# Output gates on both row halves, router rows in spare score columns: the last stage of a four-layer kernel on one core

## The chip, the core and the metric

The kernel runs on one core of a Trainium2 chip. The metric is the device time in microseconds of one execution of the whole program; three runs of the kernel before gave 1846.86, 1848.22 and 1850.99 us, median 1848.22. Engines: TensorE (PE; its weight loads are PEld), VectorE (DVE), ScalarE (ACT), GpSimd (POOL), and SyncE (SP), which here issues DMA transfers. Each runs its own queue in order.

## The reference, cut to what matters

Four residual layers work on x [16, 256, 256] (batch, tokens, features). The first three (a cross attention, a mixture of eight experts, a second cross attention) are untouched by the change. The fourth is a gated linear attention with a dense part and a part routed over four experts:

```python
e = jax.nn.softmax(x @ We, axis=-1)                  # router: 4 experts
_, idx = lax.top_k(e, 1)
mask = jax.nn.one_hot(idx, N_EXP, dtype=x.dtype).sum(-2)
rw = e * mask
...
o = o_dense + o_sparse                               # chunks of 64 tokens, 8 heads of 64
g = (x @ Wga @ Wgb).reshape(B, L, H, DV)             # output gate, 64 wide inside
o = o * lax.rsqrt(jnp.mean(o * o, axis=-1, keepdims=True) + EPS) * norm_w
o = o * (g * jax.nn.sigmoid(g))
return o.reshape(B, L, H * DV) @ Wo
```

The change concerns three things in it: the second half of the output gate (`@ Wgb` and `g * sigmoid(g)`), the turning of the router's logits (`x @ We`) from rows to columns, and the place of one product with the values.

## The kernel before

The last stage is `stage3_fast` (line 1619). It goes through 16 batches; each batch has four slots, p = 4 b + m, and in slot m the heads 2m and 2m+1 are worked on. The slots are called 0 to 3 here. Work on the next batch is spread over the slots of this one. From the first slots on every engine takes its instructions in the order in which the program issues them (`x.tied = True`): nothing is rearranged. The order within a slot is written out in the loop over p at the end and in small tables, of which these matter:

```python
behind_mask = {0: [(route_logits, 1)]}
by_rows = {0: [(outgates, 0, 0)], 1: [(gates_end, 1)], 3: [(outgates, 0, 1)]}
logs = {0: [(route_sums, 1), (outgates_end, 0, 0)], 1: [(gate_logs, 1, 0)], 2: [(gate_logs, 1, 1), (norm_ahead, 2)],
        3: [(outgates_end, 0, 1)]}
...
inside = p % 4 in (1, 2) and p + 1 < last
```

An entry (f, d, ...) calls f for the batch d ahead. A slot runs: `masked(p - 1, 1)`, `keys_queries(p + 1)`, the tables `middle`, `rest`, `decays(p + 1)`, `late`, then `products(p, 0)` (first scores, sc<-f in the profile), `masked(p, 0)` on VectorE (at<-sc,amask), `behind_mask`, `factors(p + 1)`, `by_rows`; then, where `inside` holds, `summed(p)`, the product with the values of the slot before (o<-at,v); then `second(p + 1)` (gq<-low,lbk and gz<-low,lbk), `logs`, `products(p, 1)` (second scores, sc<-q,k), and, where `inside` does not hold, `summed(p)`.

Both score groups write the same two-bank PSUM tile sc (one buffer, 384 of 512 columns used in each bank): the second may only begin when the first has been read. A head pair uses both row halves of TensorE: one head has its data on partitions 0 to 63, the other on 64 to 127. All other PSUM tiles named by `bank(...)` rotate through two buffers.

The functions the change touches:

- `lows` (line 1688), in slot 0 for the next batch: a 256-row product low, copied out of PSUM by VectorE in four operations. Rows 0 to 63 of its second part are the gate's inner values; rows 64 to 127 hold the decay gates' inner values and, from row 81 on, the router's four rows.
- `route_logits` (line 1705), in slot 0 behind the masking: two TensorE transposes bring the router's rows into the bank rt; VectorE takes their maximum (emx) and subtracts it (e), ScalarE exponentiates. `route` follows in slot 1 with seven small VectorE operations, the last of which writes hot.
- `outgates` (line 1796) and `outgates_end` (line 1808): the gate's 512 columns in two calls of two 256-column matmuls each (zg<-low,lbg), in slots 0 and 3. Their operands lie on partitions 0 to 63, so they use TensorE's lower row half alone. ScalarE computes exp(-z) (eg<-zg), then Ln and Exp of it; VectorE copies z out (zs<-zg); GpSimd multiplies (gw<-zs,eg).
- `products` (line 1892), `masked` (line 1904), `values` (line 1922), `squares` (line 1937: ScalarE's sq<-o) and `gated` (line 1946: VectorE's u<-o,gw, issued after the squares of the same o).

Matmul lines read L1637 in the profile and transposes L1640, since helpers issue them; nearly all other operations read L50.

Of the kernel before, what the change touches and what calls it, by code (L numbers as in the profile page):

```python
# [10 lines left out]
F32 = mybir.dt.float32  # L11
I32 = mybir.dt.int32
AF = mybir.ActivationFunctionType
ALU = mybir.AluOpType
# [3 lines left out]
P = 128  # L18
B, S, D = 16, 256, 256
# [7 lines left out]
def bc(ap, shape, *axes):  # L27

    for a in axes:
        ap = ap.unsqueeze(a)  # L30
    return ap.to_broadcast(list(shape))
# [42 lines left out]
def layers(ctx: ExitStack, tc: tile.TileContext, t, out, check):  # L74
    nc = tc.nc
# [6 lines left out]
    def const(name, shape, dtype=F32):  # L82
        return cp.tile(list(shape), dtype, tag=name, name=name)
# [80 lines left out]
    ident = const("ident", [P, P])  # L164
# [12 lines left out]
    dve3, act3, pool3 = free = [Pinned(tc, x, False) for x in (nc.vector, nc.scalar, nc.gpsimd)]  # L177
# [694 lines left out]
    def w3_load(name, shape, src=None):  # L872
        x = c3(name, shape)
        src = t[src or name]
        weights.append((x, src if len(src.shape) == len(shape) else src.rearrange("(k p) f -> p k f", p=P)))
        return x
# [3 lines left out]
    lbg = w3_load("lbg", [P, 512])  # L880
# [738 lines left out]
    def stage3_fast(early_bank):  # L1619

        with ExitStack() as sx:
# [3 lines left out]
            def of(b):  # L1625

                return w1 if b % 2 else w0

            def bank(name):
                return pss.tile([P, 512], F32, tag="ps", name=name) if pss else early_bank(name)  # L1630

            def tokens(i):
                return slice(i * P, (i + 1) * P)


            def matmul(*a, **k):
                tc.keep_in_program_order(nc.tensor.matmul(*a, **k))  # L1637

            def transpose(*a):
                tc.keep_in_program_order(nc.tensor.transpose(*a))  # L1640
# [1 line left out]
            halves = w1.tile([P, P], F32, tag="halves", name="halves")  # L1642
            nc.sync.dma_start(out=halves, in_=t["halves"])

            lbg2 = w1.tile([64, 512], F32, tag="lbg2", name="lbg2")
            nc.sync.dma_start(out=lbg2, in_=t["lbg"][64:P, :])
            low2 = w1.tile([64, P], F32, tag="low2", name="low2")
            wo = w1.tile([P, 4, D], F32, tag="wo", name="wo")

            hots = [w1.tile([P, 2, 4], F32, tag=f"hot{n}", name=f"hot{n}") for n in range(2)]  # L1650

            xn, xnT, low, lg, hT, em, am = {}, {}, {}, {}, {}, {}, {}
            v, gw, u_, oT = {}, {}, {}, {}


# [32 lines left out]
            def lows(b):  # L1688

                low[b] = of(b).tile([P, 2, S], F32, tag="low", name="low")  # L1690
                ps = bank("low")
                for c in range(2):
                    for k in range(2):
                        matmul(ps[:, c * S:(c + 1) * S], la[:, k, c * P:(c + 1) * P], xnT[b][:, k, :],
                                         start=k == 0, stop=k == 1)
                dve3.tensor_copy(low[b][:, 0, :], ps[:, :S])
                dve3.tensor_scalar(low[b][:, 1, :], ps[:, S:], vec[:, V_ONE:V_ONE + 1], None, ALU.add)
                if b > 0:
                    for r in range(0, 64, 32):
                        dve3.tensor_scalar(low2[r:r + 32, :], ps[64 + r:96 + r, S + P:],  # L1700
                                           vec[64 + r:96 + r, V_ONE:V_ONE + 1], None, ALU.add)

            e_, den_, z_ = {}, {}, {}

            def route_logits(b):

                ps = bank("rt")
                for i in range(2):
                    transpose(ps[:, 64 * i:64 * i + 64], low[b][64:P, 1, tokens(i)], ident[64:P, 64:P])
                src = ps[:, :P].rearrange("p (i e) -> p i e", i=2)[:, :, 17:21]  # L1710
                mx = st.tile([P, 2], F32, tag="emx", name="emx")
                dve.tensor_reduce(mx, src, AX.X, ALU.max)
                e = e_[b] = st.tile([P, 2, 4], F32, tag="e", name="e")
                dve.tensor_tensor(e, src, bc(mx, [P, 2, 4], 2), ALU.subtract)
                act.activation(e, e, AF.Exp)

            def route_sums(b):
                den = den_[b] = st.tile([P, 2], F32, tag="eden", name="eden")
                dve.tensor_reduce(den, e_[b], AX.X, ALU.add)
                dve.reciprocal(den, den)  # L1720
# [72 lines left out]
                        matmul(ps, xnT[b][:, k, tokens(i)], wv3[:, k, :], start=k == 0, stop=k == 1)  # L1793
                    act3.copy(v[b][:, i, :], ps)

            def outgates(b, i):

                if i == 0:
                    gw[b] = w2.tile([P, 4, S], F32, tag="gw", name="gw")
                ps = bank("zg")  # L1800
                for m in range(2):
                    matmul(ps[:, m * S:(m + 1) * S], lbg[0:64, (2 * i + m) * P:(2 * i + m + 1) * P],
                           low[b][0:64, 1, :], start=True, stop=True)
                e = w2.tile([P, 512], F32, tag="eg", name="eg")
                act3.activation(e, ps, AF.Exp, scale=-1.0)
                z_[b, i] = ps, e

            def outgates_end(b, i):
                ps, e = z_.pop((b, i))
                zs = w2.tile([P, 512], F32, tag="zs", name="zs")  # L1810
                dve3.tensor_copy(zs, ps)
                act3.activation(e, e, AF.Ln, bias=1.0)
                act3.activation(e, e, AF.Exp, scale=-1.0)
                pool3.tensor_tensor(gw[b][:, 2 * i:2 * i + 2, :].rearrange("p m s -> p (m s)"), zs, e, ALU.mult)


            def place(p):
                b, m = p // 4, p % 4
                return b, m, slice(m * P, (m + 1) * P)
# [72 lines left out]
            def products(p, n):  # L1892

                b, m, cols = place(p)
                q, k = fq.pop((p, n)), fk.pop((p, n))
                ps = psa.tile([P, 2, 512], F32, tag="sc", name="sc")
                for lo, hi, i in ((0, S, 0), (P, S, 1)):
                    for j in range(2):
                        r = slice(64 * j, 64 * j + 64)
                        matmul(ps[:, j, lo + i * P:hi + i * P], k[r, tokens(i)], q[r, lo:hi],  # L1900
                                         start=True, stop=True)
                z_[p, n, "sc"] = ps
# [83 lines left out]
            def warm():  # L1986

                ps = bank("warm")
                for _ in range(2):
# [3 lines left out]
            start = {2: [(turn_hot, 1)]}  # L1993
# [3 lines left out]
            rest = {0: [(bias, 2)], 1: [(route, 1)], 2: [(steepest, 1, 0), (stats, 2)], 3: [(steepest, 1, 1), (turn_ahead, 2)]}  # L1997
            late = {1: [(scaled, -1, 1)], 2: [(project, -1)], 3: [(vals, 1)]}
            behind_mask = {0: [(route_logits, 1)]}
            by_rows = {0: [(outgates, 0, 0)], 1: [(gates_end, 1)], 3: [(outgates, 0, 1)]}  # L2000
            logs = {0: [(route_sums, 1), (outgates_end, 0, 0)], 1: [(gate_logs, 1, 0)], 2: [(gate_logs, 1, 1), (norm_ahead, 2)],
                    3: [(outgates_end, 0, 1)]}

            def run(steps, p):
                for f, d, *a in steps.get(p % 4, ()):
# [4 lines left out]
                x.tied = True  # L2010
            yield
            for group in (((bias, 0), (stats, 0)), ((norm, 0),), ((turn, 0),), ((lows, 0),), ((gates, 0, 0),),
                          ((gate_logs, 0, 0), (route_logits, 0)), ((route_sums, 0), (gates, 0, 1)),
                          ((route, 0), (vals, 0), (gate_logs, 0, 1), (bias, 1))):
                for f, *a in group:
                    f(*a)
                yield
# [6 lines left out]
            w1 = sx.enter_context(tc.tile_pool(name="f3w1", bufs=1, reuse_waits="tile"))  # L2024
            w2 = sx.enter_context(tc.tile_pool(name="f3w2", bufs=2, reuse_waits="tile"))
            psa = sx.enter_context(tc.tile_pool(name="f3psa", bufs=1, space=PSUM, reuse_waits="tile"))
            pss = sx.enter_context(tc.tile_pool(name="f3ps", bufs=2, space=PSUM, reuse_waits="tile"))
            last = 4 * B
            decays(0)
            for m in range(0, 3, 2):  # L2030
                ps = bank("k2")
# [12 lines left out]
            for p in range(last):  # L2044
                if p == 0:
                    turn(1)
                run(start, p)
                if p % 4 == 0:
                    shares(p // 4)
                if 0 < p:  # L2050
                    masked(p - 1, 1)
                run(copies, p)
                if p % 4 == 0:
                    shares_end(p // 4)
                if 1 < p and p % 2 == 1:
                    gated((p - 2) // 4, (p - 2) % 4 // 2)
                if p + 1 < last:
                    keys_queries(p + 1)
                run(middle, p)
                run(rest, p)  # L2060
                if p + 1 < last:
                    decays(p + 1)
                run(late, p)
                products(p, 0)
                masked(p, 0)
                run(behind_mask, p)
                if p + 1 < last:
                    factors(p + 1)
                run(by_rows, p)

                inside = p % 4 in (1, 2) and p + 1 < last
                if inside:
                    summed(p)
                if p + 1 < last:
                    second(p + 1)
                    factors_second(p + 1)
                run(logs, p)
                products(p, 1)
                if 0 < p and not inside:
                    summed(p)  # L2080

            b, p = B - 1, last - 1
# [126 lines left out]
```

## Time and profile before

| | |
|---|---|
| median of three runs | 1848.22 us |
| the profiled execution's own time | 1848.33 us |
| its span, first to last instruction | 1846.5 us |
| TensorE busy | 1818.5 us, 98% of the span |
| VectorE busy | 1253.5 us, 68% |
| GpSimd busy | 1017.4 us, 55% |
| ScalarE busy | 858.4 us, 46% |
| zg matmul passes in the last stage | 128, 388 ns each |
| zs copies on VectorE | 32, 676 ns each |
| one batch of the last stage, steady | 38.13 us (1500.06 to 1538.19) |

How to read the lines: a timeline row gives the start in us from the span's beginning, the time it covers, engine, line, operation, the tiles as out<-in, the shape of what is moved, and how many instructions are merged in it; in brackets, idle time of the engine before it and who ended it. A row with several matmuls covers all of them, and rows overlap where matmuls are in flight together, so the distance between two starts says more than a duration. Each fp32 matmul appears as two passes, so four matmuls are "x8". `rt` writes two transposes, one pass each. The table of slots gives busy microseconds of every engine in a stretch of time, with the number of instructions.

### The profile page before, as it was taken

The numbers are of one execution on the slowest core, as the hardware profiler recorded it, in microseconds if no ns is written. First come the engines' busy times: TensorE is split into PE (matmuls) and PEld (weight loads), VectorE is DVE, ScalarE is ACT, GpSimd is POOL, SyncE is SP. The second block draws the span as 40 slices with busy tenths as digits, with TensorE's granted clock in tenths as the row PEclk, the third lists the DMA queues.
The fourth block names the chain that finished last, engine by engine and source line by source line (L and its number), as shares of the span: only waits on it lengthen the run. The fifth ranks groups of instructions, "written<-read, shape, count | busy, mean of one in ns | idle before, by whom it ended". The sixth has DMA issues, their size and how long they took to land.

```text
span 1846.5 us, 35163 instructions
## 1 busy us (share of the span) xinstructions
PE 1818.5 (98%) x13870; PEld 1258.0 (68%) x13870; DVE 1253.5 (68%) x2935; ACT 858.4 (46%) x1772; POOL 1017.4 (55%) x1001
## 2 busy tenths in 40 slices
PE   8999999999999999999999999999999999999997
PEld 5666666666766667666777766667777777777775
DVE  3355656566665666656474488878888888888875
ACT  4433344433444334443433487754545545455452
POOL 4654767567676576756634766314444444444433
PEclk9999999999999999999999999999999999999999
DMA  9800010000010000000078933000000000000000
GB/s 297 233 1 22 17 34 15 25 17 23 23 37 10 27 19 10 31 25 15 15 249 240 227 47 51 15 1 5 9 7 7 7 12 7 7 7 7 13 7 14
DMA packets 67142, 84.67 MB, mean 46 GB/s; under 512 B 10467, under 2 KB 54611, under 8 KB 66457
## 3 DMA queue, kind: packets, MB, share of 16 engines
q1 hardware_dynamic: 54681, 65.56, 11.2%
q0 software_dynamic: 12288, 16.79, 4.6%
q8 instruction: 111, 1.82, 0.4%
q14 instruction: 62, 0.51, 0.1%
HBM read 44.04 MB, written 38.29 MB: 45 GB/s over the span
## 4 chain that ended last, share of the span: by engine, by line
PE 85%; POOL 7%; DVE 4%; ACT 2%; issue 1%; DMA 1%; SPq 0%; POOLq 0%; ACTq 0%; DVEq 0%
PE o L50 11%; PE qk L50 11%; PE v L50 9%; PE sc L50 8%; PE proj L50 7%; PE kq L1637 7%; PE sc L1637 6%; POOL es L50 4%; PE gq L1637 3%; PE v L1637 3%; PE proj L1637 3%; PE o L1637 3%; PE ex L50 3%; PE gz L1637 2%; POOL rs L50 2%; PE low L1637 2%
## 5 line engine op out<-in xcount | busy, mean ns | idle before, releaser
L50 POOL TENSOR_SCALAR rs<-mv 128x2 f32<-128x2 f32 (+2 forms) x85 | 16.3, 192 | 384.4 <-DVE mv L50 380.7
L50 DVE RECIPROCAL rd<-o 128x256 f32<-128x256 f32 x64 | 112.3, 1755 | 164.1 <-PE o L50 123.7
L50 ACT ACTIVATE e<-sc 128x1024 f32<-128x1024 f32 (+1 forms) x192 | 181.6, 1016 | 18.5 <-PE sc L50 18.5
L50 PE MATMUL sc<-qk 64*128 64x256 f32 (+1 forms) x1536 | 183.1, 384 | 0.5 <-DVE qk L50 0.5
L50 PE MATMUL o<-e,v 128*32 128x256 f32 (+1 forms) x3072 | 177.9, 379 | 0.0
L50 PEld LDWEIGHTS sc<-qk 64*128 64x128 f32 (+1 forms) x1536 | 132.0, 172 | 55.1 <-issue 26.8
L50 POOL TENSOR_TENSOR esum<-esum,es 128x512 f32<-128x512 f32 x128 | 163.5, 1277 | 10.0
L50 PE MATMUL qk<-kvT,wkv 128*128 128x333 f32 x512 | 164.3, 443 | 0.0
L50 POOL TENSOR_TENSOR es<-e 128x1024 f32<-128x1024 f32 x64 | 151.3, 2364 | 12.1 <-ACT e L50 9.0
L50 ACT ACTIVATE qk<-qk 128x256 f32<-128x256 f32 x128 | 48.8, 381 | 231.4 <-PE qk L50 231.4
L50 POOL TENSOR_TENSOR at<-at,at 128x768 f32<-128x768 f32 x63 | 114.0, 1809 | 74.0 <-DVE at L50 73.3
L50 POOL TENSOR_TENSOR es<-es,e 77x1024 f32<-77x1024 f32 x64 | 150.4, 2351 | 5.0
L50 PEld LDWEIGHTS o<-e,v 128*32 128x32 f32 (+1 forms) x3072 | 99.9, 110 | 66.3
L50 PE MATMUL qk<-kvT,wq 128*128 128x256 f32 x512 | 134.6, 385 | 0.0
L50 DVE COPY qk<-qk 128x333 f32<-128x333 f32 x128 | 64.6, 504 | 93.8 <-ACT qk L50 92.8
L50 POOL DMA_INDIRECT x<-rows_out,pos x64 | 101.0, 1578 | 35.3 <-issue 18.8
L50 PEld LDWEIGHTS qk<-kvT,wq 128*128 128x128 f32 x512 | 94.3, 189 | 35.1 <-issue 9.6
L50 PEld LDWEIGHTS qk<-kvT,wkv 128*128 128x128 f32 x512 | 97.2, 190 | 30.0
L50 PE MATMUL proj<-wo0h,oT 128*128 128x256 f32 x512 | 113.7, 380 | 0.3 <-DVE oT L50 0.3
L50 PE MATMUL v<-wkv,kvT 128*128 128x512 f32 x256 | 113.1, 594 | 0.0
L50 POOL TENSOR_TENSOR gw<-zs,eg 128x512 f32<-128x512 f32 x32 | 40.8, 1274 | 120.4 <-ACT eg L50 120.4
L50 PEld LDWEIGHTS proj<-wo0h,oT 128*128 128x128 f32 x512 | 95.9, 190 | 13.9 <-issue 0.8
(259 smaller groups left out, 4110.3 us busy)
## 6 DMA issues: line engine op xcount, KB each, us to landing
rows<-zero SPq DMA_DIRECT2D x16, 640.0 KB
xin<-rows SPq DMA_DIRECT2D x16, 640.0 KB
rows_out<-y SPq DMA_DIRECT2D x16, 384.0 KB
v<-vctx SPq DMA_DIRECT2D x15, 308.0 KB
x<-in_x_dram SPq DMA_DIRECT2D x16, 256.0 KB
rows_out<-y SPq DMA_DIRECT2D x16, 256.0 KB
out_dram<-x SPq DMA_DIRECT2D x15, 256.0 KB
wkv<-in_wkv_dram SPq DMA_DIRECT2D x2, 1024.0 KB
```

The costliest lines, as they stand in the source:

```text
L50: x = getattr(self.engine, name)(*a, **k)
L1637: tc.keep_in_program_order(nc.tensor.matmul(*a, **k))
```

## The change

- `outgates` is called once per batch, in slot 0, for all four column blocks. Blocks 0 and 2 use low and lbg on partitions 0 to 63 as before and write one bank; blocks 1 and 3 use copies on partitions 64 to 127 and write another. The copy of the weights (`lbg2`, upper half) is loaded once; the copy of low (`lowd`) is made for every batch by a DMA on SP's queue, right behind `lows`.
- ScalarE now does both reads of each zg bank: exp, and the copy zs that was VectorE's. `outgates_end` runs for the two banks in slots 0 and 1.
- The router's transposes are issued at the head of `products(p, 0)` in slot 0, and write columns 384 to 511 of the second bank of sc; emx and e read them there. The bank rt is no longer used in the loop.
- `inside` holds in slot 3 as well: `values` of slot 2 comes before the second scores.

```diff
-            lbg2 = w1.tile([64, 512], F32, tag="lbg2", name="lbg2")
-            nc.sync.dma_start(out=lbg2, in_=t["lbg"][64:P, :])
+            lbg2 = w1.tile([P, 512], F32, tag="lbg2", name="lbg2")
+            nc.sync.dma_start(out=lbg2[:64], in_=t["lbg"][64:P, :])
+            nc.sync.dma_start(out=lbg2[64:], in_=t["lbg"][:64, :])
...
                 dve3.tensor_scalar(low[b][:, 1, :], ps[:, S:], vec[:, V_ONE:V_ONE + 1], None, ALU.add)
+                lowd[b] = of(b).tile([P, S], F32, tag="lowd", name="lowd")
+                nc.sync.dma_start(out=lowd[b][64:], in_=low[b][:64, 1, :])
...
+            def route_rows(b, ps):
+
+                for i in range(2):
+                    transpose(ps[:, 64 * i:64 * i + 64], low[b][64:P, 1, tokens(i)], ident[64:P, 64:P])
+                z_["rt"] = ps
+
             def route_logits(b):
 
-                ps = bank("rt")
-                for i in range(2):
-                    transpose(ps[:, 64 * i:64 * i + 64], low[b][64:P, 1, tokens(i)], ident[64:P, 64:P])
-                src = ps[:, :P].rearrange("p (i e) -> p i e", i=2)[:, :, 17:21]
+                ps = z_.pop("rt")
+                src = ps.rearrange("p (i e) -> p i e", i=2)[:, :, 17:21]
...
-            def outgates(b, i):
-
-                if i == 0:
-                    gw[b] = w2.tile([P, 4, S], F32, tag="gw", name="gw")
-                ps = bank("zg")
-                for m in range(2):
-                    matmul(ps[:, m * S:(m + 1) * S], lbg[0:64, (2 * i + m) * P:(2 * i + m + 1) * P],
-                           low[b][0:64, 1, :], start=True, stop=True)
-                e = w2.tile([P, 512], F32, tag="eg", name="eg")
-                act3.activation(e, ps, AF.Exp, scale=-1.0)
-                z_[b, i] = ps, e
-
-            def outgates_end(b, i):
-                ps, e = z_.pop((b, i))
-                zs = w2.tile([P, 512], F32, tag="zs", name="zs")
-                dve3.tensor_copy(zs, ps)
+            def outgates(b):
+
+                gw[b] = w2.tile([P, 4, S], F32, tag="gw", name="gw")
+                two = [bank("zg"), bank("zg")]
+                for i in range(2):
+                    for h, (w, x) in enumerate(((lbg[0:64], low[b][0:64, 1, :]), (lbg2[64:], lowd[b][64:]))):
+                        m = 2 * i + h
+                        matmul(two[h][:, i * S:(i + 1) * S], w[:, m * P:(m + 1) * P], x, start=True, stop=True)
+                for h, ps in enumerate(two):
+                    e, zs = (w2.tile([P, 512], F32, tag=n, name=n) for n in ("eg", "zs"))
+                    act3.activation(e, ps, AF.Exp, scale=-1.0)
+                    act3.copy(zs, ps)
+                    z_[b, h] = zs, e
+
+            def outgates_end(b, h):
+                zs, e = z_.pop((b, h))
                 act3.activation(e, e, AF.Ln, bias=1.0)
                 act3.activation(e, e, AF.Exp, scale=-1.0)
-                pool3.tensor_tensor(gw[b][:, 2 * i:2 * i + 2, :].rearrange("p m s -> p (m s)"), zs, e, ALU.mult)
+                pool3.tensor_tensor(gw[b][:, h::2, :], *(x.rearrange("p (m s) -> p m s", m=2) for x in (zs, e)), ALU.mult)
...
                 ps = psa.tile([P, 2, 512], F32, tag="sc", name="sc")
+                if n == 0 and m == 0 and b + 1 < B:
+                    route_rows(b + 1, ps[:, 1, 384:])
...
-            by_rows = {0: [(outgates, 0, 0)], 1: [(gates_end, 1)], 3: [(outgates, 0, 1)]}
-            logs = {0: [(route_sums, 1), (outgates_end, 0, 0)], 1: [(gate_logs, 1, 0)], 2: [(gate_logs, 1, 1), (norm_ahead, 2)],
-                    3: [(outgates_end, 0, 1)]}
+            by_rows = {0: [(outgates, 0)], 1: [(gates_end, 1)]}
+            logs = {0: [(route_sums, 1), (outgates_end, 0, 0)], 1: [(outgates_end, 0, 1), (gate_logs, 1, 0)], 2: [(gate_logs, 1, 1), (norm_ahead, 2)]}
...
-                inside = p % 4 in (1, 2) and p + 1 < last
+                inside = p % 4 > 0 and p + 1 < last
```

More of the change, by code (lines that the diff above doesn't have):

```diff
@@ L1650, in stage3_fast @@
             hots = [w1.tile([P, 2, 4], F32, tag=f"hot{n}", name=f"hot{n}") for n in range(2)]
-            xn, xnT, low, lg, hT, em, am = {}, {}, {}, {}, {}, {}, {}
+            xn, xnT, low, lg, hT, em, am, lowd = {}, {}, {}, {}, {}, {}, {}, {}
             v, gw, u_, oT = {}, {}, {}, {}
@@ L1703, in stage3_fast, with route_logits @@
             e_, den_, z_ = {}, {}, {}
-            def route_logits(b):
-                ps = bank("rt")
+            def route_rows(b, ps):
                 for i in range(2):
                     transpose(ps[:, 64 * i:64 * i + 64], low[b][64:P, 1, tokens(i)], ident[64:P, 64:P])
-                src = ps[:, :P].rearrange("p (i e) -> p i e", i=2)[:, :, 17:21]
+                z_["rt"] = ps
+            def route_logits(b):
+                ps = z_.pop("rt")
+                src = ps.rearrange("p (i e) -> p i e", i=2)[:, :, 17:21]
                 mx = st.tile([P, 2], F32, tag="emx", name="emx")
@@ L1715, in route_logits, with route_first @@
                 act.activation(e, e, AF.Exp)
+            def route_first(b):
+                route_rows(b, bank("rt")[:, :P])
+                route_logits(b)
             def route_sums(b):
@@ L2012, in stage3_fast @@
             for group in (((bias, 0), (stats, 0)), ((norm, 0),), ((turn, 0),), ((lows, 0),), ((gates, 0, 0),),
-                          ((gate_logs, 0, 0), (route_logits, 0)), ((route_sums, 0), (gates, 0, 1)),
+                          ((gate_logs, 0, 0), (route_first, 0)), ((route_sums, 0), (gates, 0, 1)),
                           ((route, 0), (vals, 0), (gate_logs, 0, 1), (bias, 1))):
```

## The prediction

> **What bounds the kernel now.** I read the page's busy rows first, then busy time by slot, then the timeline of TensorE, then that of VectorE. The page:
>
> ```profile
> PE 1818.5 (98%) x13870; PEld 1258.0 (68%) x13870; DVE 1253.5 (68%) x2935; ACT 858.4 (46%) x1772; POOL 1017.4 (55%) x1001
> PEclk9999999999999999999999999999999999999999
> ```
>
> TensorE is busy throughout at full clock. I call the four slots of a batch 0 to 3 (p % 4; the title's slot one is slot 0, its slot four slot 3). Busy time of slots 0 to 3 of one steady batch, cut where each slot's first score matmul starts:
>
> ```profile
> core 0: us, PE busy (x) PEld busy (x) DVE busy (x) ACT busy (x) POOL busy (x), PEclk, DMA share, GB/s
> 1500.06:1508.80 8.74, 8.74 (x62) 6.03 (x61) 8.16 (x23) 5.33 (x14) 3.76 (x3) 1.00 0.01 2
> 1508.80:1519.17 10.37, 10.37 (x68) 8.24 (x67) 6.53 (x16) 4.96 (x13) 4.98 (x7) 1.00 0.00 0
> 1519.17:1529.22 10.05, 10.05 (x56) 6.42 (x55) 9.47 (x23) 6.00 (x13) 4.57 (x5) 1.00 0.08 28
> 1529.22:1538.19 8.97, 8.97 (x65) 7.09 (x64) 7.87 (x17) 2.94 (x7) 4.49 (x4) 1.00 0.00 0
> ```
>
> Every slot is filled by TensorE; VectorE follows at 93% in slot 0. So a batch (38.13 us) shrinks only by what leaves TensorE's row, and any new wait on VectorE between the two score groups of a slot adds to it. TensorE in slot 2, then in slot 3 and the start of slot 0:
>
> ```profile
> 1519.17 0.92 PE L1637 MATMUL sc<-f 64*128 64x256 f32 x8
> 1520.02 0.87 PE L1637 MATMUL o<-at,v 128*64 128x256 f32 x8
> 1520.82 0.48 PE L1637 MATMUL gq<-low,lbk 64*128 64x256 f32 x1
> 1520.83 0.48 PE L1637 MATMUL gz<-low,lbk 64*128 64x256 f32 x1
> ...
> 1521.36 0.82 PE L1637 MATMUL sc<-q,k 64*128 64x256 f32 x8
> ...
> 1529.22 0.92 PE L1637 MATMUL sc<-f 64*128 64x256 f32 x8
> 1529.97 0.81 PE L1637 MATMUL zg<-low,lbg 64*128 64x256 f32 x3
> ...
> 1530.84 0.59 PE L1637 MATMUL gq<-low,lbk 64*128 64x256 f32 x2
> 1531.43 0.92 PE L1637 MATMUL sc<-q,k 64*128 64x256 f32 x8
> 1532.28 0.87 PE L1637 MATMUL o<-at,v 128*64 128x256 f32 x8
> 1533.08 0.64 PE L1637 MATMUL den<-e,halves 128*32 128x256 f32 x8
> ```
>
> Read: gq and gz, on different row halves, start 0.01 us apart and run side by side. Slot 2 puts o between the score groups and needs 2.19 us from sc<-f to sc<-q,k; slot 3 puts zg there, needs 2.21, and has o as 0.80 us more behind. Now slot 0, VectorE beside TensorE:
>
> ```profile
> 1537.75 1.23 DVE L50 TENSOR_SCALAR low<-low,vec 128x256 f32<-128x256 f32 x3
> 1538.19 0.92 PE L1637 MATMUL sc<-f 64*128 64x256 f32 x8
> 1538.85 0.25 PEld L1640 LDWEIGHTS rt<-ident,low 64*128 64x128 f32 x2
> 1539.23 0.96 DVE L50 TENSOR_TENSOR at<-sc,amask 128x768 f32<-128x768 f32 x1 [0.26 <-PE rt L1640]
> 1540.11 0.15 DVE L50 TENSOR_REDUCE emx<-rt 128x2 f32<-128x8 f32 x1
> 1540.30 0.17 DVE L50 TENSOR_TENSOR e<-rt,emx 128x8 f32<-128x8 f32 x1
> 1540.35 0.92 PE L1637 MATMUL sc<-q,k 64*128 64x256 f32 x8
> ```
>
> The first of the three low rows (0.48 us, done at 1538.23) makes the router's rows. It ends while sc<-f already runs, so rt at 1538.85 finds it ready; sc<-q,k waits for at (done 1540.19), not for emx and e.
>
> **Slot 3: what goes.** The whole zg group leaves, and o takes its place. sc<-f to sc<-q,k becomes slot 2's 2.19; today it is 2.21 and the last pass comes still later: at ended at 1531.28, the weight load behind it came at 1531.40 and the real start near 1531.50, where slot 2's pattern gives about 1531.43. Gain 0.07. o's 0.80 behind the group is gone; den follows sc<-q,k. o is covered by data: its POOL sum at of the slot before ends at 1525.5, four us early. den needs e from gz, now last before it: by slot 2's rows e is done 2.8 us after sc<-f and den is due at 2.9, so I take off 0.02 at most. Sum **-0.85 us** per batch (bounds -0.75 and -0.95).
>
> **Slot 0: four zg on both halves.** Today two zg matmuls (two passes each) and gq queue on the low half: six passes of 0.216 us. Afterwards the low half has the same six (zg m 0 and 2, then gq); m 1 and 3 run on the high half beside them, as gq/gz show. Price on TensorE 0.
>
> **Slot 0: router rows first.** The two rt transposes move ahead of sc<-f. They need low at 1538.23; a single-wait load follows VectorE by 0.05 (slot 2 of the first batch: at ended 1254.20, load at 1254.25), so 1538.28 instead of the 1538.19 at which sc<-f loads now. From rt's load to the following group's load is 0.18 (1538.85 to 1539.03). sc<-f is thus late by 0.09 + 0.18 = **0.27**. A rule speaks against more than that row: the Trainium skill (TensorEngine Tiling, Key Properties) says that changing the tiling mode drains TensorE. The drain shows as 0.20 us between the last gz<-em pass and the sc<-f load. If a transpose counts as a mode of its own, there is one more drain, and the delay is 0.47. But rt is 64x128 as are its neighbours, and zg follows rt today with 0.07 lost: I take 0.27 and keep 0.47 for the range.
>
> **Slot 0: the new wait.** emx and e now read the score buffer, and there is one such buffer: sc<-q,k has to wait for e. e ends 1.23 after at's start (1540.47 today), so at 1540.74 with the 0.27. Behind a several-fold wait the load came 0.12 after VectorE in slot 3 (1531.28 to 1531.40); this one has three conditions, so 0.12 to 0.17. Load 1540.86 to 1540.91, first pass 0.11 later: 1540.97 to 1541.02, where it now is 1540.45 (single passes). Slot 0 costs **+0.53 in all** (0.27 included). On TensorE alone it would be 0.08: 0.27 less the 0.19 that rt no longer takes before zg. Behind sc<-q,k queue all TensorE work of the slot, so this is paid in full.
>
> **ScalarE and what follows it.** ScalarE gets four reads of zg in slot 0 (eg, zs, eg, zs at 0.47 apart, from eg's row spacing 1502.48 to 1502.95), then e<-gz (0.27), Ln and Exp (1.20), then sq. From e's end at 1540.74: eg 1540.89, e<-gz 1542.77, Ln 1543.04, sq 1544.24 to 1544.82; today sq starts 4.36 after sc<-f, then 6.05. VectorE's u reads o after sq, so it waits on ScalarE until 1544.87; behind it stand the seven router steps to hot, then slot 1's first masking. gw moves to 1544.36-1545.63 on POOL, the sum at to 1545.63-1547.44. The router's e<-e,eden has two SBUF inputs. By the Trainium skill (SBUF, Who interferes with whom) it blocks fully against a POOL operation under way and issue order decides: caught behind gw and at it would end at 1547.49, and hot at 1548.69. The nearest row speaks for less: in the first batch it took 0.55 us, slipping in between gw and at, and the next one (eq, 1.54 us) waited at out. I take that: hot at 1547.44 + 0.82 = 1548.26. Slot 1's masking is due at 1546.94 + 0.53 + 1.04 = 1548.51: 0.25 to spare, price **0**; by the rule's worst reading +0.2.
>
> **The rest.** zs leaves VectorE (32 x 0.676 = 21.6 us) with no price or gain: VectorE waits for TensorE around it. The 16 lowd transfers go through SP. No SBUF-to-SBUF transfer stands in the trace; they are 64 KB against the 256 KB of out_dram<-x, issued in slot 0 and used four slots (38 us) later. In SP's queue they stand ahead of out_dram<-x, which waits until slot 2 anyway. Cover gone, each would stall zg by its landing. The one extra lbg2 load stands before loads that run ahead: 0 (bound 0.3 once). POOL's gw of slot 3 moves to slot 1, between k (done 1512.92) and the sum at, which then ends at 1516.0 instead of 1515.2; o needs it at 1520.02: 0.
>
> **Sum.** -0.85 + 0.53 = -0.32 per batch; 15 batches have both parts: -4.8. The last batch has no router and loses zg in slot 3, where masking (at) then bounds: -0.1. Total **-4.9 us** on the profiled 1848.33 (span 1846.5 and 1.8 around it), which is 0.11 over the median 1848.22; from the median: 1843.3.
>
> **Rivals.**
> - *Only TensorE's own work counts* (the wait for e hidden, because the buffer is released by at): slot 0 costs 0.08, -0.77 x 15 = -11.5: 1836.7. For it: TensorE is 98% busy. Against: at already ends only 0.15 before sc<-q,k starts, and e comes 0.28 after at.
> - *The transposes are a mode of their own* and the three-fold wait takes 0.17: +0.25, -0.07 x 15 = -1: 1847.
> - *Slot 1's masking comes late: slower.* Place: ScalarE's queue in slot 0 holds sq, so u, so hot. If ScalarE's four reads run at their full 0.59 instead of 0.47 (+0.44 to sq) and e is caught behind both POOL operations (+0.43), hot is 0.87 later, 0.62 beyond its slack: +0.30 x 15 = +4.5: 1852.7. It decides from hot 0.57 us later than worked out (0.25 slack and the 0.32 gained). Against: the spacings are those of rows that queue back to back.
>
> **How the numbers follow.** Likeliest 0.52; TensorE alone or half-way to it 0.11; own mode 0.24; slower 0.13. A measurement tells 0.2% (3.7 us) from no change: faster than 1844.5 is most of the likeliest and the first rival, 0.60; the rest of the likeliest and the mode case are within it, 0.27; slower 0.13. The likeliest case alone runs from 1840.5 to 1845.5 (bounds of slot 3 and of the wait). The range 1838.0 to 1850.0 reaches half-way into both outer rivals.
>
> **What would show it.** Right: batch period 37.8; in slot 3 no zg, sc<-q,k 2.2 after sc<-f, then den; in slot 0 rt, then sc<-f near 0.3 late, eight zg in pairs, sc<-q,k 2.4 after sc<-f with e as releaser; u preceded by a wait for sq of 1.6 us. Wrong: sc<-q,k at 2.2 in slot 0 (too timid), a gap before sc<-q,k in slot 1 (hot too late), a load gap of 0.2 after rt, or zg on the two halves one after the other (+0.86).

## The result and the profile after

The changed kernel takes 1844.38 us (median of 12 runs, 1841.46 to 1847.08) against 1849.56 of the kernel before (12 runs beside it, 1846.86 to 1851.17): ratio 0.9968, 95% interval 0.9959 to 0.9976, or 5.2 us less. The forecast was 1843.3 and 4.9 less. The profiled execution took 1847.08, 2.7 over that median; its span is 1845.3, and the busy rows on its page read:

```profile
PE 1813.5 (98%) x13870; PEld 1249.8 (68%) x13870; DVE 1231.5 (67%) x2903; ACT 873.9 (47%) x1804; POOL 1017.0 (55%) x1001
```

The spans of the two profiled executions differ by 1.2 us only. Cut at the first score matmul of batch 0, the rest of the program is 604.88 us now and was 609.64, so 4.8 less. What precedes the cut is 3.5 longer, in code that the change hardly touches. Three stretches of the new execution show where the rest of the gain went (the third column from the end is the granted clock):

```profile
1056.20:1063.00 6.80, 6.68 (x56) 3.10 (x60) 4.23 (x7) 3.45 (x8) 4.96 (x5) 0.50 0.53 71
1213.20:1216.60 3.40, 3.40 (x12) 2.22 (x15) 3.07 (x3) 1.07 (x4) 0.00 (x0) 0.51 0.02 5
1824.20:1827.60 3.40, 3.40 (x20) 2.50 (x22) 1.94 (x5) 0.00 (x0) 0.85 (x1) 0.50 0.00 0
```

TensorE had work and half its clock, for 10.2 us ahead of the cut (up to 5.1 lost) and 3.4 in the last slot of the program. The kernel before has clock 1.00 at all three places. The last slot is 1.37 longer than before (23.35 against 21.98); in the kernel with the rows second, below, which has the same last slot and full clock there, it is 21.98. The first 15 batches are 6.1 shorter than before; less 3.5 and 1.4 that is the 1.2 of the spans.

A run's time goes with its granted clock too. Of the kernel before, 73 runs beside the experiments have their mean granted clock on record: at 0.998 the median is 1848.03 (15 runs), at 0.996 it is 1851.17 (25). The changed kernel has 1841.96 at 0.998 (3 of its 12 runs) and 1844.94 at 0.996 (5). So at the same clock the change is worth 6.1 to 6.2 us (5.6 and 5.8 at 0.999 and 0.997, from 2 runs and 1), as the batches say. What the change does is therefore read below from the batches, not from the spans. All slots are measured from a slot's first pass to the next slot's first pass, as means over the 13 steady batches (us):

| kernel | slot 0 | slot 1 | slot 2 | slot 3 | batch |
|---|---|---|---|---|---|
| before | 8.74 | 10.37 | 10.05 | 8.98 | 38.14 |
| after | 9.12 | 10.37 | 10.05 | 8.18 | 37.72 |

The first pass of a slot 0 is late in itself, and that lateness stands at the end of slot 3: the table's 0.80 is 0.89 gained less 0.09 of slot 0's cost (shown in an experiment below). Slot 3 of the changed kernel, TensorE:

```profile
1530.39 0.92 PE L1637 MATMUL sc<-f 64*128 64x256 f32 x8
1531.24 0.87 PE L1637 MATMUL o<-at,v 128*64 128x256 f32 x8
...
1532.58 0.85 PE L1637 MATMUL sc<-q,k 64*128 64x256 f32 x8
1533.36 0.64 PE L1637 MATMUL den<-e,halves 128*32 128x256 f32 x8
```

zg is gone, o stands between the score groups, sc<-q,k starts 2.19 us after sc<-f, and den follows it. Now slot 0, VectorE beside TensorE:

```profile
1538.03 1.22 DVE L50 TENSOR_SCALAR low<-low,vec 128x256 f32<-128x256 f32 x3
...
1538.56 0.14 PEld L1640 LDWEIGHTS sc<-ident,low 64*128 64x128 f32 x1 [0.21 <-DVE low L50]
...
1538.57 0.48 PE L1637 MATMUL sc<-f 64*128 64x256 f32 x1
...
1539.72 0.96 DVE L50 TENSOR_TENSOR at<-sc,amask 128x768 f32<-128x768 f32 x1 [0.46 <-PE sc L1637]
...
1540.78 0.17 DVE L50 TENSOR_TENSOR e<-sc,emx 128x8 f32<-128x8 f32 x1
...
1541.10 0.92 PE L1637 MATMUL sc<-q,k 64*128 64x256 f32 x8 [0.19 <-DVE e L50]
```

The transposes wait for low; sc<-f's passes on the other row half start 0.01 after the first of them; at starts 1.14 after the first pass (1.04 before); and sc<-q,k waits for e, 2.52 after the first pass instead of 2.15. The last gz pass began at 1540.53, so, with 0.216 us to a pass, TensorE stands for about 0.35 us. Behind that, VectorE up to slot 1's masking:

```profile
1545.11 0.69 DVE L50 TENSOR_TENSOR u<-o,gw 128x512 f32<-128x512 f32 x1 [1.66 <-ACT sq L50]
1545.72 0.24 DVE L50 TENSOR_TENSOR e<-e,eden 128x8 f32<-128x8 f32 x1
...
1546.19 1.55 DVE L50 TENSOR_TENSOR eq<-e,em 128x8 f32<-128x8 f32 x1
...
1548.73 0.96 DVE L50 TENSOR_TENSOR at<-sc,amask 128x768 f32<-128x768 f32 x1 [0.19 <-PE sc L1637]
```

u waits 1.66 us for sq on ScalarE, eq for POOL's sum (1545.89 to 1547.71), and still VectorE is idle 0.19 us ahead of the masking: slot 1 stays at 10.37.

### The profile page after: what moved, and what is told of

Same layout as the page of the kernel before. It is cut to its first block, busy times and chain, and to the rows that moved or that the text cites. A ratio compares the mean times of both kernels' runs of the same rounds, so it can differ in the third digit from the quotient of the medians.

```text
span 1845.3 us, 35182 instructions
## 1 busy us (share of the span) xinstructions
PE 1813.5 (98%) x13870; PEld 1249.8 (68%) x13870; DVE 1231.5 (67%) x2903; ACT 873.9 (47%) x1804; POOL 1017.0 (55%) x1001
## 4 chain that ended last, share of the span: by engine, by line
PE 82%; POOL 9%; DVE 4%; issue 2%; ACT 2%; DMA 1%; SPq 0%; POOLq 0%; DVEq 0%; ACTq 0%
PE o L50 11%; PE qk L50 11%; PE v L50 8%; PE sc L50 8%; PE proj L50 7%; PE kq L1637 7%; PE sc L1637 5%; POOL es L50 4%; PE gq L1637 3%; PE v L1637 3%; PE o L1637 3%; PE proj L1637 3%; POOL x L50 2%; PE ex L50 2%; POOL rs L50 2%
## 5 line engine op out<-in xcount | busy, mean ns | idle before, releaser
L50 POOL DMA_INDIRECT rows<-xw,pos x64 | 66.8, 1043 | 61.1 <-ACT xT L50 24.0
```

The source lines that it names most:

```text
L50: x = getattr(self.engine, name)(*a, **k)
```

## The experiments

Each is one edit of the changed kernel unless said otherwise. Times are medians; a ratio is to the kernel before, beside it on the same chip, with its 95% interval. Batches (us), from the profiled execution of each:

| kernel | median us (runs) | ratio | slot 0 | slot 1 | slot 3 | batch |
|---|---|---|---|---|---|---|
| values behind | 1856.85 (5) | 1.0039 (1.0024 to 1.0054) | 9.12 | 10.37 | 9.08 | 38.61 |
| low half only | 1845.99 (9) | 0.9985 (0.9975 to 0.9995) | 9.40 | 10.39 | 8.18 | 38.03 |
| rows in own bank | 1855.62 (5) | 1.0043 (1.0029 to 1.0056) | 10.23 | 10.37 | 8.09 | 38.73 |
| rows second | 1838.80 (5) | 0.9942 (0.9929 to 0.9956) | 8.90 | 10.37 | 8.09 | 37.40 |
| copies on VectorE | 1847.48 (20) | 0.9991 (0.9983 to 1.0000) | 9.37 | 10.37 | 8.18 | 37.97 |
| copies twice | 1860.51 (9) | 1.0048 (1.0033 to 1.0064) | 9.34 | 11.07 | 8.18 | 38.64 |
| rows second, low half | 1848.31 (20) | 0.9989 (0.9981 to 0.9997) | 9.41 | 10.37 | 8.11 | 37.93 |
| rows second, paired | 1838.07 (6) | 0.9940 (0.9922 to 0.9958) | 8.83 | 10.37 | 8.09 | 37.34 |
| low rows swapped | 1840.76 (6) | 0.9953 (0.9938 to 0.9969) | 9.12 | 10.37 | 8.09 | 37.63 |

Slot 2 is 10.05 in all of them. Two means hold one odd slot each: in low half only one slot 1 took 10.69 (the others 10.37, their batches 38.00), in rows second, low half one slot 3 took 8.37 (8.09, 37.91). Most medians come from few runs whose clocks differ, so the batches are the finer measure.

**Values behind again.**

```diff
-                inside = p % 4 > 0 and p + 1 < last
+                inside = p % 4 in (1, 2) and p + 1 < last
```

> One part undone: in slot 3 the value products o go behind sc<-q,k again; everything else of the change stays. Theory (o covers the wait between the score groups, and the 0.80 us it no longer costs behind them is the gain): slot 3 goes from 8.18 to about 8.95 to 9.0 us, because between sc<-f and sc<-q,k only gq and gz are left, 0.4 us of work, and sc<-q,k still cannot start before at, 2.1 us after sc<-f. Batch period 38.45 to 38.5 instead of 37.72, that is longer than the 38.13 of the kernel before; time +11 to +12 us over the changed kernel, about 1856. Rival (the gain comes from pairing the four zg on both row halves, and where o stands is indifferent): slot 3 stays near 8.2, period 37.7, time 1844.

Slot 3 is 9.08, the batch 38.61, even 0.47 longer than before the change. The 0.47 is slot 0's cost: less the 0.09 that slot 0's late start puts at its end, slot 3 is back at the 8.98 of the kernel before. The theory holds, with 0.1 more than it said. TensorE in slot 3:

```profile
1653.40 0.92 PE L1637 MATMUL sc<-q,k 64*128 64x256 f32 x8 [0.85 <-DVE at L50]
```

With o behind, TensorE is idle 0.85 us before sc<-q,k (gq and gz are all that is left), and o is paid in full afterwards. So o inside slot 3 is worth 0.90 a batch: it fills a wait that taking zg away would have opened.

**All zg on the low half.**

```diff
-                    for h, (w, x) in enumerate(((lbg[0:64], low[b][0:64, 1, :]), (lbg2[64:], lowd[b][64:]))):
+                    for h, (w, x) in enumerate(((lbg[0:64], low[b][0:64, 1, :]), (lbg[0:64], low[b][0:64, 1, :]))):
```

(with lowd and the upper half of lbg2 taken out)

> One part undone: all four zg of slot 0 take their rows from the low row half (lowd and the upper half of lbg2 are gone), into the same two banks in the same order. Theory (the halves run side by side, so the two zg on the high half were free): the low half has ten passes of 0.216 us instead of six, +0.86 us on TensorE between sc<-f and sc<-q,k in slot 0; some 0.3 to 0.45 of that hides in the wait for e that is there now, so sc<-q,k starts 2.95 to 3.1 us after sc<-f instead of 2.52, and the period is 38.15 to 38.3 (+0.45 to +0.6), time +7 to +9 us over the changed kernel. Rival (pairing pays nothing, or the wait for e covers all of it): period 37.7, time the same. Rival (the wait for e is no cover): the full +0.86, +13 us.

Pairing pays, but only 0.28 a batch in slot 0, less than the theory's 0.45 to 0.6. TensorE (slot 0's first pass is at 1535.27):

```profile
1537.87 0.41 PE L1637 MATMUL sc<-q,k 64*128 64x256 f32 x1
1537.97 0.38 PE L1637 MATMUL gq<-low,lbk 64*128 64x256 f32 x1
1538.12 0.88 PE L1637 MATMUL sc<-q,k 64*128 64x256 f32 x7
```

sc<-q,k starts at 2.60 on the high half, whose own queue is short, while the low half still has gq; the group's last pass starts at 3.46 instead of 3.17. (The trace doesn't name the half of a pass; it is read from the order and the spacing.) The row halves run here as two queues, and the group is over with the slower. Of the low half's 0.86, its wait for e (0.47: its last gq pass ended at about 2.05, sc<-q,k came at 2.52) and a wider step behind the wait (0.29 between its first two passes where 0.216 is usual) hid 0.55; 0.03 more was free, as the high half's last pass had come that much later than its own.

**The rows in a bank of their own.**

```diff
-                if n == 0 and m == 0 and b + 1 < B:
-                    route_rows(b + 1, ps[:, 1, 384:])
...
+                if n == 0 and m == 0 and b + 1 < B:
+                    route_rows(b + 1, bank("rt")[:, :P])
```

> One part undone: the router's rows are transposed behind sc<-f into a bank of their own, as before the change, so that sc<-q,k need not wait for e; zg on both halves and values inside slot 3 stay. Theory (the spare score columns are what keeps a rotating bank free): the own bank is one of two that rotate, and the second zg bank becomes the one that e still reads; zg on the high half waits for e at about 2.3 us after sc<-f, and all of zg, gq and sc<-q,k stand behind it. sc<-q,k at about 3.7 instead of 2.52, slot 0 +1.1 to +1.2, period 38.8 to 38.9, time +15 to +18 us. Rival (the bank is free in time and only the wait of sc<-q,k for e goes): sc<-q,k near 2.2, period 37.3 to 37.4, time -5 to -6 us.

The theory holds in the main: slot 0 is 10.23, 1.11 longer, although sc<-f starts on time (slot 3 8.09) and sc<-q,k no longer waits for e; sc<-q,k starts at 3.35, earlier than the 3.7 that was said. The batches add up to 15 us, the low end of the 15 to 18; the medians give 11. TensorE:

```profile
1618.80 0.70 PE L1637 MATMUL zg<-low,lbg 64*128 64x256 f32 x2
1620.33 0.45 PE L1637 MATMUL zg<-lowd,lbg 64*128 64x256 f32 x1 [0.84 <-issue]
```

The first zg goes into the free bank; the second needs the bank that e reads, e ends at 1620.24, and all that follows stands behind it. So the spare score columns, and the wait for e with them, are the cheaper of two waits for the same reader.

**The rows in the second score group.**

```diff
-                if n == 0 and m == 0 and b + 1 < B:
+                if n == 1 and m == 0 and b + 1 < B:
...
-            copies = {2: [(turned_hot, 1)]}
+            copies = {1: [(route_logits, 1), (squares, -1, 1), (route_sums, 1)], 2: [(turned_hot, 1)]}
-            behind_mask = {0: [(route_logits, 1)]}
+            behind_mask = {}
-            logs = {0: [(route_sums, 1), (outgates_end, 0, 0)], ...
+            logs = {0: [(outgates_end, 0, 0)], ...
...
-                if p % 2 == 0:
+                if p % 4 == 2:
```

> The router's rows go into the spare columns of slot 0's second score group (sc<-q,k) instead of the first; emx, e and eden are read in slot 1 ahead of squares, which moves there too. Theory (the cost of the change in slot 0 is the wait for low, the transposes ahead of sc<-f and the wait of sc<-q,k for e; all three go): sc<-q,k about 2.15 to 2.25 us after sc<-f, slot 0 8.75 to 8.85 instead of 9.12, period 37.35 to 37.45, time -4 to -6 us under the changed kernel, about 1839. Rival (the wait only moves: emx, e and the router's steps now stand on VectorE ahead of slot 1's first masking, at is late there): slot 1 +0.3 to +0.8 instead, period 37.7 to 38.2, time +0 to +6 us. Rival (e was no cost in slot 0, something else holds sc<-q,k): slot 0 stays at 9.1.

The batch is 37.40, 0.32 shorter, and the time 1838.80: the theory's numbers, and faster than both kernels. Slot 0 is 8.90, above the 8.75 to 8.85, and slot 3 gives the 0.09 of the lead back. TensorE in slot 0:

```profile
1607.72 0.48 PE L1637 MATMUL sc<-q,k 64*128 64x256 f32 x1
1607.89 0.28 PE L1640 MATMUL sc<-ident,low 64*128 64x64 f32 x2
```

sc<-q,k starts 2.06 after sc<-f with no wait for e; the transposes hold only the high half. Slot 1 keeps 10.37 with 0.67 us idle on VectorE before its masking, so the rival falls in the steady batches. In the first batch it is right: there the masking of slot 1 starts at 1.73 instead of 0.97, and that slot is 7.56 against 7.22.

**Pairing without the wait.** The same with all zg on the low half.

> All four zg on the low row half, as in the run that undid the pairing, but now with the router's rows in the second score group, so that sc<-q,k does not wait for e. There the four extra passes (0.86 us on the low half) cost 0.28 us a batch. Theory (0.45 us of them hid in the wait for e, the rest behind the weight loads after it): without the wait the low half is late by 0.86, less the 0.15 to 0.2 that the transposes hold the high half; slot 0 at 9.55 to 9.65 instead of 8.90, period 38.05 to 38.15, time +10 to +11 us over the kernel with the rows in the second group, near 1849. Rival (pairing is worth 0.28 by itself, since the row halves queue apart and the high half makes up for it): slot 0 at 9.2, time +4 us.

Slot 0 is 9.41, +0.51: between the two. The low half's last pass comes 0.75 later (2.71 to 3.46), not 0.86: in the kernel with the rows second its first two sc<-q,k passes are 0.32 apart, though no wait precedes them, and here 0.216 (why is not shown). And 0.25 of that was free, since in the kernel with the rows second the high half ended last (2.95), behind the transposes. The same four passes thus cost 0.28 or 0.51 by what the other half and the wait do. The theory had the mechanism, and took the high half's lead too small.

**The two transposes side by side**, on the rows-second kernel: token half 0 as before into one bank, token half 1 from low2 on the low half into the other.

```diff
-                for i in range(2):
-                    transpose(ps[:, 64 * i:64 * i + 64], low[b][64:P, 1, tokens(i)], ident[64:P, 64:P])
+                if b > 0:
+                    transpose(ps[:, 1, :], low[b][64:P, 1, tokens(0)], ident[64:P, 64:P])
+                    transpose(ps[:, 0, :], low2, ident[:64, :64])
```

> On top of the kernel with the rows in the second score group: of the two transposes of a batch, that of the second token half takes its rows from low2 (the same values, on the low row half) and goes into the other bank, so that the two run side by side on both row halves; the router then holds its token halves in swapped order and the turn of hot swaps them back. Theory (there the high half's last sc<-q,k pass ends 0.25 us after the low half's, because both transposes stand on it; a group is over when its slower half is): each half takes one transpose, slot 0 at 8.75 to 8.8 instead of 8.90, period 37.25 to 37.3, time -1.5 to -2.2 us, near 1837. Rival (two transposes side by side cost each half as much as both cost one, by their weight loads): slot 0 stays at 8.9, time the same.

Slot 0 is 8.83, 0.06 less, some half of what the theory said (why only half is not shown); the time, 0.7 us less, can't be told from none. The group's last pass is at 2.89 instead of 2.95.

**VectorE's order at low.** Back on the changed kernel:

```diff
-                dve3.tensor_copy(low[b][:, 0, :], ps[:, :S])
                 dve3.tensor_scalar(low[b][:, 1, :], ps[:, S:], vec[:, V_ONE:V_ONE + 1], None, ALU.add)
+                dve3.tensor_copy(low[b][:, 0, :], ps[:, :S])
```

> The changed kernel with one order turned: VectorE writes the rows of low that the transposes read before the other rows of low instead of after, so that they are there 0.3 to 0.4 us earlier. Theory (the start of slot 0 is late by 0.09 us because the transposes wait for low; the rest of the cost of slot 0 is the wait for e): slot 3 ends at 8.09 instead of 8.18, at of slot 0 starts 1.04 to 1.14 us after the first pass as now, slot 0 stays at 9.12 or up to 0.05 more, period 37.63 to 37.68, time -0.6 to -1.4 us. Rival (the transposes themselves push sc<-f back, not the wait): nothing changes.

As the theory says, to the hundredth: slot 3 is 8.09, slot 0 stays 9.12, the batch is 37.63. The row that the transposes read:

```profile
1607.17 0.48 DVE L50 TENSOR_SCALAR low<-low,vec 128x256 f32<-128x256 f32 x1 [0.73 <-PE low L1637]
```

It is done at 1607.65, the transposes load at 1607.95, and at still starts 1.14 after the first pass. So the wait for low costs 0.09 and the transposes ahead of sc<-f 0.10. The median is 3.6 under the changed kernel's, more than 15 times 0.09. Part of that goes with the clock: these six runs had 0.997 to 0.999, the changed kernel's twelve 0.995 to 0.999, and at the same clock the two differ by 1 to 2 us (15 x 0.09 is 1.3).

**The copies zs on VectorE.**

```diff
-                    act3.copy(zs, ps)
+                    dve3.tensor_copy(zs, ps)
```

> One part undone: the two copies zs of slot 0 run on VectorE instead of ScalarE (0.676 us each, as before the change, but both in slot 0). Theory (ScalarE only sets when sq, u and hot come, and hot has 0.2 us to spare; u waits 1.66 us for sq on VectorE, so VectorE has room for 1.35 us of copies if ScalarE gives sq 0.9 us earlier): the price is nothing either way, slot 0 at 9.1, slot 1 at 10.37, period 37.7, time within 2 us of the changed kernel. Rival (VectorE is the next bound of slot 0, 93% busy there before the change): q1 or the router's steps come later by the copies, sc<-q,k of slot 0 or the masking of slot 1 is late by 0.3 to 0.7, time +4 to +10 us.

Neither: slot 1 keeps 10.37 and sc<-q,k of slot 0 its 2.52, but slot 0 is 0.25 longer at its end. VectorE, then TensorE:

```profile
1616.22 1.37 DVE L50 SCALAR_TENSOR_TENSOR at<-sc,kden,am 128x256 f32<-128x256 f32 x4
```

```profile
1617.38 0.70 PE L1637 MATMUL z<-lbg,low 17*128 17x512 f32 x2
1617.65 0.70 PE L1637 MATMUL sc<-lbg,low 17*128 17x512 f32 x2
```

The copies push the second masking back by 1.45 us (4.94 after the first pass instead of 3.49). Its reads hold the score buffer until 1617.59, and the next batch's gates, half of which go into that buffer, start their pairs 0.27 apart instead of 0.02. That the masking holds them up is inferred from its end and the start 0.06 behind it.

**The copies twice**, where the prediction's slower rival has its place.

```diff
+                    act3.copy(zs, ps)
                     act3.copy(zs, ps)
```

> One suspected cost doubled: each of the two copies zs of slot 0 is made twice on ScalarE (two more reads of zg, 0.94 us more in its queue; the output is the same). This is the place that the slower rival of the prediction named. Theory (sq, u, gw and the sum at on POOL all come 0.94 later, hot with them; the masking of slot 1 has 0.19 us to spare): at of slot 1 is 0.7 to 0.8 late and sc<-q,k behind it; o of slot 1 may be late by about as much. Slot 1 at 11.0 to 11.15 instead of 10.37, time +10 to +12 us. Rival (the slack is larger than it looks, because VectorE slips in between POOL's operations and catches up): slot 1 stays within 0.2 us of 10.37, time 0 to +3 us.

The theory holds: slot 1 is 11.07, +0.70. VectorE at its start:

```profile
1634.10 0.17 DVE L50 TENSOR_TENSOR hot<-eq,e 128x8 f32<-128x8 f32 x1
1634.19 0.95 DVE L50 TENSOR_TENSOR at<-sc,amask 128x768 f32<-128x768 f32 x1
```

The masking follows hot without a gap, 1.77 after sc<-f instead of 1.04. Slot 0 grows by 0.22 besides, which was not expected: ms<-sq starts at 1631.36, 0.05 after ScalarE's read lg<-z has ended (1630.72 + 0.59), whose bank it seems to take. It comes 0.11 later in its slot than in the changed kernel and takes 0.10 longer, which makes the 0.22; no run tests this reading. With it the batches add up to 15 us, above the 10 to 12 that were said, and the medians give 16.

## Why the prediction was right, step by step

- **Slot 3, -0.85: measured -0.89.** sc<-q,k at 2.19 as said. The run with o behind gives +0.90 back. The late masking was worth 0.09 instead of 0.07 (the group's last pass starts at 2.77 instead of 2.87), and the 0.02 taken off for den did not come: den follows without a stall.
- **Router rows first, +0.27: measured +0.19.** This is a term that was mis-sized. The wait for low is the 0.09 that was worked out (low done 1538.51, load 1538.56). The 0.18 for the transposes was taken from rt's load to the next group's load in a place where rt stood in the middle of a full row half; at the head of the slot the other half's sc<-f passes start beside them, and they cost 0.10. The rival "a mode of its own" falls with it: by the Trainium skill (TensorEngine Tiling, Key Properties) a change of mode drains TensorE, and no drain stands between a transpose and a score pass of the same 64x128 shape (loads at 1538.56 and 1538.57).
- **The new wait for e: +0.53 for all of slot 0; measured 0.46** (0.38 in slot 0, 0.09 ahead of it, rounded). e ended 1540.95, 2.38 after the first pass; the load came 0.11 behind it, where 0.12 to 0.17 was said, and the pass at 0.15. Less the 0.19 above, the wait for e is 0.27 of the sum, where 0.26 was said; the 0.07 too much are the transposes' 0.08. Taking wait and transposes away (rows second) gives 0.32 back.
- **Four zg on both halves, 0 on TensorE: right** as far as the low half has the same six passes. Undone, they cost 0.28 under the wait for e and 0.51 without it.
- **ScalarE's queue, price 0: right**, by 0.19 us of slack where 0.25 was worked out. u waited 1.66 (said: 1.6). By the Trainium skill (SBUF — State Buffer, Who interferes with whom) e<-e,eden could have been caught by POOL; it began at 1545.72, was done at 1545.96 between gw (to 1545.94) and the sum, and the next two-input step, eq, took 1.55, ending with POOL's sum. This fits the issue order: e<-e,eden began 0.17 ahead of the sum, eq 0.30 behind its start. The worst reading of the rule, behind both POOL operations, did not come, and the nearest row was the better guide.
- **zs off VectorE, "no price or gain": too short.** Against the kernel before, where one copy stood in slot 0 and one in slot 3, no run tests it. With both in slot 0 the move counts: on VectorE they cost 0.25 a batch.
- **lowd's transfers, 0: right**; zg<-lowd starts 0.12 behind zg<-low with no wait shown.
- **Sum, -0.32 x 15: measured -0.42 in a steady batch**, -5.5 in 13 of them. The first batch gave only 0.16 (34.14 against 34.30), since its slot 1 is 7.22 instead of 6.91: POOL's gw comes behind ScalarE's longer queue, its sum ends at 1249.46, and o waits 0.24 for it, where the prediction had looked at o only in the steady batches. The batch before the last gave 0.48. The last batch, put at -0.1, gives nothing: its first three slots are unchanged, and its last is 21.98 before and with the rows second, at full clock.
- **The slower rival** did not come: ScalarE's reads start 0.46 to 0.49 apart, as forecast, e<-e,eden slipped in, and hot was 0.19 ahead of its use. "Copies twice" shows that its place was real: 0.94 us on ScalarE's queue, less 0.19, is 0.75, and slot 1 grew by 0.70.

The batches alone give 13 x 0.42 + 0.16 + 0.48 = 6.1 us, the ratio's interval 4.4 to 7.6. The forecast of 4.9 lies inside because its errors are terms of under 0.1 us (transposes 0.08 and slot 3 0.04 a batch), and the first batch gave back 0.26 of them. Both errors point the same way, so the mechanism gives 1.2 us more than was said; that the medians differ by 5.2, nearer to 4.9, is luck of the runs' clocks.

## What to carry to other kernels

Work taken out from between two dependent groups only pays if other ready work takes its place; here o, which fills the wait for the masking, is worth 0.90 us a batch, and without it the same removal gains nothing in its slot. When a result is parked in a buffer that others need, count its reader as a new holder of that buffer and put it behind the last group that writes it: the same rows cost 0.46 in the first score group, 1.5 in a rotating bank and 0.15 in the second group (slot 0 with the 0.09 ahead of it, against the kernel before). An engine that waits has slack only as far as the next use of what it makes: 0.94 us more on ScalarE's queue, behind which VectorE waited 1.66, cost 0.92.

## What was not expected of the hardware

- The granted clock fell to half in stretches of 3.4 and 6.8 us in which TensorE was busy 98 to 100%; the 3.4 us ahead of the three in the changed kernel's execution had it busy 1.52, 2.23 and 1.73. How busy it was just ahead doesn't decide alone: the kernel with the rows second has the same 1.73 at the same place of its last slot and keeps full clock. Of the eleven profiled executions three had such a stretch ahead of batch 0 (after, values behind, copies twice) and reached it at 1239.1 to 1240.4 us; the eight others at 1234.5 to 1236.9. That moves a span by as much as the change. Why it falls in one execution and not in another is open.
- The row halves drain apart: a score group on one half starts up to 0.32 us ahead of the other (2.60 and 2.92 with all zg on the low half), and later work starts with the slower. Passes on different halves even start out of the order in which the kernel issues them: with the rows second, the transposes are issued ahead of sc<-q,k and start 0.17 behind its first pass (1607.89 and 1607.72). A single busy row for TensorE doesn't show it.
- A VectorE step with two SBUF inputs took 0.24 us in the gap between two POOL operations and 1.46 to 1.73 when it came while POOL's sum ran (1.55 here, 1.73 in the kernel before); the one-input reduction between them, 0.16, ran beside POOL.
